# Doubles of two pairs as the unit of the main loop in a four-layer graph network kernel

## The chip, the cores and the metric

One core of a Trainium2 chip runs the whole kernel; the other cores do nothing. The metric is the device time of one execution in microseconds. The engines are called PE (matrix multiply), DVE (vector), ACT (activation), POOL (GpSimd) and SP (which issues most DMAs). Each works through its own instructions in order and waits for the others by semaphores.

## The reference

There are 128 graphs of 64 nodes with 128 features each (`x`), and one 64 x 64 matrix of edge distances per graph (`adj`), symmetric in its pattern, with about a quarter of its entries not zero. Four layers follow one another, each with a residual and a layer norm:

```python
# layer 0: continuous filter, 20 Gaussians, cosine cutoff
f_ij = exp(coeff * (d_ij[..., None] - offsets) ** 2)
rcut = 0.5 * (cos(d_ij * pi / CUTOFF) + 1.0) * (d_ij < CUTOFF)
W = (ssp(f_ij @ fw1 + fb1) @ fw2 + fb2) * rcut[..., None]
agg = einsum('bjf,bijf->bif', x @ w_in2f, W)
out = ssp(agg @ ow1 + ob1) @ ow2 + ob2

# layer 1: the same with 64 Gaussians; the edges are weighted with A * A
# layer 2: graph convolutions with the normalised adjacency
h = elu(elu(x @ W0 + b0))
h = elu(norm_A @ (h @ W1) + b1)
out = norm_A @ (h @ W2) + b2

# layer 3: out = relu((A_norm @ X) @ W.T + b)
# each layer: x = layernorm(x + out)
```

`ssp` is softplus minus log 2. In layers 0 and 1 the filter `W` is computed for every edge, which is nearly all the work. Everything is float32.

## The kernel before

**Tiling.** The graphs are sorted by their number of edges and taken in pairs: 64 pairs in 8 sets of 8. For each pair the edges are compacted into *slots*; the number of slots of a pair is fixed by its set (948 to 1092 in layer 0, 1140 to 1260 in layer 1, constant `GSLOTS`). Slots are ordered by the nodes they belong to, so that the sum over the edges of a node is a reduce over a stretch of neighbouring slots. The compaction of the first set is done ahead of the main loop; that of the later sets runs in small portions beside the loop (queues `early` and `side`), on DVE, POOL and through indirect DMAs.

**The loop.** `n` counts 128 pairs, 64 of layer 0 and then 64 of layer 1. A pair is cut into three steps of a third of its slots (316 to 364 columns in layer 0, 380 to 420 in layer 1; both graphs of a pair are handled in one step, so an ACT or DVE instruction has twice as many elements). A step is a pipeline over three iterations:

- `filter_in` (L1791): `px`, the matmul of the Gaussians `d` with the first filter weights, for two halves of 64 rows; then ACT's exponential into `h`. In layer 0 the three thirds of a pair lie on different rows of `d`, each with its own copy of the weights in `fw1`.
- `softplus`: ACT's logarithm of `h`, in place.
- `gather` (L1817), one iteration later: `pg`, the matmul of the node features with the selection matrix `hot`; then ACT's copy into `g`.
- `filter_out` (L1805), two iterations later: `pw`, the second filter matmul. All ACT instructions are recorded at L933.
- `message` (L1831): DVE computes `(pw + b2) * g` into the pair's messages `m`.
- `slot_sums` (L1854, L1858): 9 reduces on DVE from `m` into `agg`, once per pair, spread over the following steps.

`px`, `pg` and `pw` have one PSUM tile of two banks each, without a second buffer. So the next `px` waits for the exponential, the next `pg` for the copy and the next `pw` for the message. `one_hot` (L1779) builds `hot` on DVE from slot numbers and edge weights `w`.

**Beside the loop.** Pairs form groups of four (`GS`). A group's node work is in generators that yield between pieces; each step runs one piece of each queue: `befores` (features for the next group), `nodes` (`node_after`: `u` at L1581, softplus, `o`, un-sorting `back`, residual, layer norm) and the two queues `convs` (`graph_convs`: layers 2 and 3 of one group each, taken in turn by the group's number). In layer 0, `zero_share` adds what the entries with weight but no edge bring: a DVE instruction (L1554) adds it to `agg` just before `u`. Normal matrices of the convolutions are built by POOL (`scaled`, L1646) and transposed by PE (`nT`). POOL also does the layer norms' scaling (L1441) and scatters finished rows to the output. The last groups of layer 1 have 4, 2, 1 and 1 pairs, so that the end after the last step is short. The order of the instructions on each engine is the order in which this loop records them (`in_order`); the number of pieces of each queue at each step is written out by hand:

```python
        run(sums, ((1, 4, 4), (2, 4, 5))[n >= NP][k])
        run(early, 9 if i < 18 else (PACE - 2, PACE + 1, PACE + 1)[k] if i < 3 * (NP - 8) else 7)
        run(side, min(2, len(side)))
        run(stores, 1)
```

Loads of a pair (`d`, then `j` and `w`) are issued two pairs ahead: `d` at its step 0, `j` and `w` at step 1.

Of the kernel before, what the change touches and what calls it, by code (L numbers as in the profile page):

```python
# [19 lines left out]
P = 128  # L20
# [46 lines left out]
CHUNKS = tuple(tuple(n // 3 for n in sizes) for sizes in GSLOTS)  # L67
MAX_SLOTS, MAX_CHUNK = max(map(max, GSLOTS)), max(map(max, CHUNKS))

# [532 lines left out]
def sparse_stack(ctx: ExitStack, tc: tile.TileContext, t: dict, out: bass.AP, flag):  # L602
# [24 lines left out]
    dram = ctx.enter_context(tc.tile_pool(name="sscratch", bufs=1, space=DRAM))  # L627
    edge = ctx.enter_context(tc.tile_pool(name="sedge", bufs=2))
# [55 lines left out]
    columns = const.tile([P, P], F32, name="columns")  # L684
    column_i = const.tile([P, P], I32, name="column_i")
# [55 lines left out]
    def load_terms(name):  # L741
# [4 lines left out]
        yield  # L746
# [22 lines left out]
    fw1 = const.tile([P, 3, C], F32, name="fw1")  # L769
# [73 lines left out]

    def count(v, pool, total):
# [63 lines left out]
    caps_row = const.tile([1, NS, 2, 9], F32, name="caps_row")  # L908
# [7 lines left out]
    compacting = ctx.enter_context(ExitStack())  # L916
    cpt = compacting.enter_context(tc.tile_pool(name="scompact", bufs=1, side="right"))
# [377 lines left out]
    def bounded():  # L1295
# [11 lines left out]
        yield from wait_steps(8 * PACE)  # L1307
        for i, (w1, b1) in enumerate(loaded):
            nc.vector.scalar_tensor_tensor(w1, w1, -1.0, w1, ALU.mult, ALU.max)
            nc.vector.scalar_tensor_tensor(b1, b1, -1.0, b1, ALU.mult, ALU.max)  # L1310
            yield from wait_steps(2 * PACE)
            u = ps_n.tile([P, 512], F32, tag="n", name=f"sum_{i}")
            nc.tensor.matmul(u[:, 0:1], lhsT=w1, rhs=one[0 : w1.shape[0]], start=True, stop=True)
            nc.vector.tensor_add(b1, b1, u[:, 0:1])
# [3 lines left out]
    def settle():  # L1318
# [8 lines left out]
        yield from wait_steps(2 * PACE)  # L1327
        u = ps_n.tile([P, 512], F32, tag="n", name="odd_sum")
        nc.tensor.matmul(u[0:1, 0:3], lhsT=one, rhs=odds, start=True, stop=True)
        sums_ = const.tile([1, 3], F32, name="odd_sums")  # L1330
        nc.vector.tensor_copy(sums_, u[0:1, 0:3])
# [9 lines left out]
    def later_loads(n):  # L1341
# [9 lines left out]
        w = edge.tile([P, MAX_SLOTS], F32, tag="w", name=f"w_{n}")  # L1351
# [65 lines left out]
    def once(name, n, q):  # L1417

        if n < GS and rings:
            return tiled(name, n, q)  # L1420
        return node.tile([P, GS * P], F32, tag=name, name=f"{name}_{q}", bufs=1)[:, 0 : n * P]

    def layernorm(y, dst, n, name):

        stats = node.tile([P, GS, 6], F32, tag="st", name=f"st_{name}")[:, 0:n]
        mv = node.tile([P, GS, 2], F32, tag="mv", name=f"mv_{name}")[:, 0:n]
        for s in range(n):
            nc.vector.bn_stats(stats[:, s, :], y[:, s, :])
            nc.vector.bn_aggr(mv[:, s, :], stats[:, s, :])  # L1429
            if s + 1 == GS // 2 < n:  # L1430
                yield
        rstd = node.tile([P, GS], F32, tag="rs", name=f"rs_{name}")[:, 0:n]
# [624 lines left out]
```

## Time and profile before

| | us |
|---|---|
| median of 3 runs | 1589.59 |
| lowest and highest of them | 1589.56, 1591.46 |
| the profiled execution | 1576.21 |
| its span, first to last instruction | 1574.4 |
| PE, DVE, ACT, POOL busy in the span | 1435.9, 1365.7, 1335.9, 763.7 |
| first `px` of the main loop begins at | 67.9 |
| layer 0, pairs in eight sets | 67.9 to 726.4 |
| layer 1, pairs in eight sets | 726.4 to about 1500 |

The profile is of one execution, which was 13.4 us shorter than the median. Times inside it are counted from its first instruction. A row of the groups names the line, engine and operation, what is written and read, the shape, how many there are, the time that they keep the engine busy, the mean of one in ns, and the engine's idle time just before them with what ended it. One float32 matmul is recorded as two matmul rows. The chain of waits follows the end of the program back, at each step to what released it. PE's granted clock was 0.984 of full speed.

### The profile page before, as it was taken

To read this page: it belongs to the slowest core of one execution; us is meant where nothing else is said; L and a number is where in the kernel's file an instruction comes from. 1 tells how busy PE (TensorE), PEld (TensorE's weight loads), DVE (VectorE), ACT (ScalarE), POOL (GpSimd) and SP (SyncE) were. 2 spreads that over 40 slices of the span, in tenths; PEclk is the share of its full clock that TensorE was granted. 3 is DMA by queue.
4 is the path that set the end of the run, shared out by engine and by line. 5 is a ranking of instruction groups with operands and counts; after the bars stand their busy time and mean duration, and the time that the engine had idled before them with its cause. 6 is when DMAs were issued, how large, how long until landed. Compare 5 with 4: busy or idle time off the path is not lost.

```text
span 1574.4 us, 24209 instructions
## 1 busy us (share of the span) xinstructions
PE 1435.9 (91%) x6813; PEld 812.1 (52%) x6813; DVE 1365.7 (87%) x3549; ACT 1335.9 (85%) x1846; POOL 763.7 (49%) x1175
## 2 busy tenths in 40 slices
PE   1379999999999999999999999999999999999975
PEld 1134455555555555554445555555555655555554
DVE  8789999999999998889878888888888887898873
ACT  1369898989898988889999999999999998999952
POOL 2434356555655635335521346544565444664454
PEclk9999999999999999999999999999999999999985
DMA  6755455545454643437565455544555454555200
GB/s 207 256 132 145 128 125 148 129 128 141 121 140 122 151 125 100 129 100 185 142 151 130 122 148 131 144 124 124 137 134 138 120 132 128 131 143 132 70 8 23
DMA packets 122290, 205.68 MB, mean 131 GB/s; under 512 B 47956, under 2 KB 80034, under 8 KB 121506
## 3 DMA queue, kind: packets, MB, share of 16 engines
q1 hardware_dynamic: 113330, 188.40, 46.8%
q0 software_dynamic: 6576, 14.99, 2.8%
q8 instruction: 57, 0.93, 0.3%
q10 hardware_dynamic: 2240, 0.65, 0.2%
q14 instruction: 87, 0.71, 0.2%
HBM read 185.29 MB, written 18.64 MB: 130 GB/s over the span
## 4 chain that ended last, share of the span: by engine, by line
PE 33%; DVE 21%; POOL 13%; DMA 10%; ACT 9%; issue 6%; SPq 3%; DVEq 0%; POOLq 0%; ACTq 0%
PE pw L1805 12%; PE px L1791 7%; DVE m L1831 6%; PE pg L1817 5%; DMA out_dram<-gz,at_row 5%; POOL x_all L1441 5%; ACT h L933 4%; DVE agg L1854 4%; DVE hot L1779 2%; POOL rs L1436 2%; SPq L1354 2%; POOL gz L1441 2%; DMA w<-w_dram 2%; ACT g L933 2%; PE hw L1689 1%
## 5 line engine op out<-in xcount | busy, mean ns | idle before, releaser
L933 ACT ACTIVATE h<-h,half 128x672 f32<-128x672 f32 (+13 forms) x385 | 353.7, 919 | 0.1
L933 ACT ACTIVATE g<-pg 128x672 f32<-128x672 f32 (+12 forms) x384 | 303.8, 791 | 28.0 <-DVE m L1831 18.6
L1854 DVE TENSOR_REDUCE agg<-m 128x16 f32<-128x240 f32 (+13 forms) x896 | 319.6, 411 | 2.9
L1817 PE MATMUL pg<-hot,ys 64*128 64x336 f32 (+12 forms) x1536 | 308.8, 478 | 12.8 <-DVE hot L1779 9.6
L1805 PE MATMUL pw<-h,w_L_gnn_W2T 128*128 128x420 f32 (+5 forms) x768 | 306.2, 521 | 1.6 <-DVE m L1831 1.6
L1831 DVE SCALAR_TENSOR_TENSOR m<-pw,c_L_gnn_b,g 128x840 f32<-128x840 f32 (+5 forms) x192 | 201.3, 1048 | 104.5 <-PE pw L1805 95.4
L1805 PE MATMUL pw<-h,w_L_gnn_fw 128*128 128x336 f32 (+6 forms) x768 | 264.6, 467 | 21.3 <-DVE m L1831 20.1
L1805 PEld LDWEIGHTS pw<-h,w_L_gnn_W2T 128*128 128x128 f32 x768 | 130.3, 189 | 148.5 <-issue 32.6
L1831 DVE SCALAR_TENSOR_TENSOR m<-pw,c_L_gnn_fb,g 128x672 f32<-128x672 f32 (+6 forms) x192 | 176.9, 921 | 33.4 <-PE pw L1805 21.6
L933 ACT ACTIVATE h<-px,c_L_gnn_fb 128x672 f32<-128x672 f32 (+6 forms) x192 | 159.5, 830 | 53.5 <-PE px L1791 53.2
L1817 PEld LDWEIGHTS pg<-hot,ys 64*128 64x128 f32 x1536 | 146.0, 187 | 113.6 <-issue 17.8
L933 ACT ACTIVATE h<-px,c_L_gnn_b 128x840 f32<-128x840 f32 (+5 forms) x192 | 178.8, 931 | 26.0 <-PE px L1791 25.4
L1791 PE MATMUL px<-d,fw 64*128 64x336 f32 (+6 forms) x768 | 165.7, 506 | 28.9 <-ACT d L933 18.8
L1805 PEld LDWEIGHTS pw<-h,w_L_gnn_fw 128*128 128x128 f32 x768 | 132.8, 191 | 112.8 <-DVE m L1831 65.1
L1779 DVE SCALAR_TENSOR_TENSOR hot<-j,row,w 128x1212 f32<-128x1212 bf16 (+12 forms) x128 | 177.9, 1390 | 7.4 <-DMA d<-d_dram 7.4
L1791 PE MATMUL px<-d,w1t 64*128 64x420 f32 (+5 forms) x768 | 181.1, 548 | 1.1 <-ACT h L933 1.1
L1435 POOL TENSOR_SCALAR rs<-mv 128x4 f32<-128x4 f32 x61 | 14.7, 240 | 305.1 <-DVE mv L1429 303.1
L933 ACT ACTIVATE d<-d,neg_off 128x1212 f32<-128x1212 f32 (+12 forms) x128 | 120.3, 940 | 9.0 <-DMA d<-d_dram 9.0
L1791 PEld LDWEIGHTS px<-d,fw 64*128 64x128 f32 x768 | 59.5, 187 | 120.8 <-ACT h L933 48.9
L973 POOL DMA_INDIRECT rows<-comb,goes x64 | 67.8, 1060 | 96.7 <-DMA rows<-comb,goes 66.6
L1441 POOL TENSOR_SCALAR x_all<-ny,mv,rs 128x128 f32<-128x128 f32 x124 | 105.4, 859 | 3.3
L973 POOL DMA_INDIRECT out_dram<-gz,at_row x56 | 78.6, 1403 | 13.9 <-POOL blocks L1646 4.5
(262 smaller groups left out, 2243.8 us busy)
## 6 DMA issues: line engine op xcount, KB each, us to landing
d<-d_dram SPq DMA_DIRECT2D x32, 315.0 KB
w<-w_dram SPq DMA_DIRECT2D x32, 315.0 KB
d<-d_dram SPq DMA_DIRECT2D x32, 303.0 KB
w<-w_dram SPq DMA_DIRECT2D x32, 303.0 KB
w<-w_dram SPq DMA_DIRECT2D x32, 252.0 KB
j<-j_dram SPq DMA_DIRECT2D x32, 157.5 KB
j<-j_dram SPq DMA_DIRECT2D x32, 151.5 KB
d<-d_dram SPq DMA_DIRECT2D x16, 300.0 KB
```

The costliest lines, as they stand in the source:

```text
L933: latest = nc.scalar.activation(out_, in_, func, **kw)
L973: nc.gpsimd.indirect_dma_start(out=into, out_offset=bass.IndirectOffsetOnAxis(ap=at, axis=0), in_=rows, in_offset=None,)
L1354: engine.dma_start(to, dram_ap(slots[layer, name][s], first, [[0, to.shape[0]], [1, n]]))
L1436: nc.gpsimd.tensor_tensor(rstd, rstd, neg_half[:, 0:n], ALU.pow)
L1441: (nc.gpsimd if n == GS else nc.vector).tensor_scalar(dst[:, s, :], y[:, s, :], mv[:, s, 0:1], rstd[:, s : s + 1], ALU.subtract, ALU.mult,)
L1689: nc.tensor.matmul(ps[:, s, :], lhsT=lhs(s), rhs=rhs(s), start=True, stop=True)
L1779: nc.vector.scalar_tensor_tensor(hots[n][:, 0:size], j[:, 0:size], near, wt[:, 0:size], ALU.is_equal, ALU.mult)
L1791: nc.tensor.matmul(ps[:, b, 0:n], lhsT=w1, rhs=d[rows, col : col + n], start=True, stop=True)
L1805: nc.tensor.matmul(c["pw"][:, b, :], lhsT=c["w"]["w2"], rhs=c["h"][:, b, :], start=True, stop=True)
L1817: nc.tensor.matmul(ps[:, b, 0:n], lhsT=y[rows, :], rhs=hots[c["n"]][rows, at], start=True, stop=True,)
L1831: nc.vector.scalar_tensor_tensor(messages[n][:, :, at], c["pw"], c["w"]["b2"], c["g"], ALU.add, ALU.mult)
L1854: nc.vector.tensor_reduce(av[:, :, :, r], both, AX.X, ALU.add)
```

## The change

The unit of the loop becomes a *double* of two neighbouring pairs.

- **Steps.** In layer 1 a double is cut into 5 steps of about two fifths of a pair's slots (456 to 504 columns); the middle one takes the end of the first pair and the beginning of the second. In layer 0 a double is cut into 4 steps of half a pair where a pair has up to 1024 slots (sets 3 to 7, 474 to 510 columns), otherwise into 6 as before. `filter_in` and `gather` issue one pair of matmuls for each piece with its own weights or its own pair.
- **In place.** `hot` is written over `w` (three buffers instead of two). ACT copies `pg` straight into the double's messages `m`, and DVE multiplies there.
- **Sums.** The 9 reduces run once for a double, over twice as many elements each; only the last double is summed pair by pair. `agg` is single-buffered.
- **Zero share.** It is no longer added to `agg`: ACT writes the scaled share (`zz`), and `u` is computed in four matmuls, in layer 0 in four pairs of matmuls that accumulate share and sums. The share's work moves to the queue `befores`.
- **Turns.** How many pieces of each queue a step runs, and at which step loads and Gaussians are issued, comes from a table for 6, 5 and 4 steps. `graph_convs` of a large group waits for given steps of a group (`at_phase`), and `befores` runs at given steps alone. The two normal matrices are built within `elu` while ACT works. Some layer norms run in fewer pieces.

The core of the diff:

```diff
+def chunks_of(layer, size):
+    if layer == 1:
+        wide = -(-2 * size // 5)
+        return (wide, wide, size - 2 * wide, size - 2 * wide, wide, wide)
+    n = 2 if size <= 1024 else 3
+    return (size // n,) * (2 * n)
...
-        w = edge.tile([P, MAX_SLOTS], F32, tag="w", name=f"w_{n}")
+        w = edge.tile([P, MAX_SLOTS], F32, tag="w", name=f"w_{n}", bufs=3)
...
     def zero_share(q):
...
-        nc.vector.scalar_tensor_tensor(agg, ps, zero_filter, agg, ALU.mult, ALU.add)
+        shares[q] = once("zz", GS, q)
+        act(shares[q], flat, AF.Identity, scale=zero_filter)
...
-        nc.tensor.matmul(
-            u, lhsT=w["o1"], rhs=agg.rearrange("f s r -> f (s r)"), start=True, stop=True
-        )
+        for s in range(n):
+            of = agg[:, s, :]
+            if n > 1:
+                of = agg[:, s // 2 * 2 : s // 2 * 2 + 2, :].rearrange("f s r -> f (s r)")
+                of = of.rearrange("f (b s r) -> f s b r", b=2, s=2)[:, s % 2]
+            if layer == 0:
+                nc.tensor.matmul(by[:, s, :], lhsT=w["o1"], rhs=share[:, s, :], start=True, stop=False)
+            nc.tensor.matmul(by[:, s, :], lhsT=w["o1"], rhs=of, start=layer == 1, stop=True)
...
         if n == GS:
+            yield from at_phase(6)
             scaled(2, q)
...
-        hots[n] = edge.tile([P, MAX_SLOTS], F32, tag="hot", name=f"hot_{n}")
+        hots[n] = wt
...
+    def pieces(c):
+        at = 0
+        for part_ in c["parts"]:
+            first, stop = part_["cols"]
+            third = stop if c["layer"] else part_["all"] // 3
+            while first < stop:
+                k = first // third
+                end = min(stop, (k + 1) * third)
+                yield part_, k, first - k * third, at, end - first
+                at, first = at + end - first, end
...
+        for to, of in c["to"]:
+            act(to, ps[:, :, of], AF.Copy)
+
+    def message(c):
+        for to, of in c["to"]:
+            nc.vector.scalar_tensor_tensor(
+                to, c["pw"][:, :, of], c["w"]["b2"], to, ALU.add, ALU.mult
+            )
...
+        v = m.rearrange("f (g k) -> f g k", g=8 * pairs)
...
+    TURNS = {
+        6: dict(
+            sums=(1, 1, 2, 1, 2, 2), early=(PACE - 2, PACE + 1, PACE + 1) * 2, side=(2,) * 6,
+            late=(2, None, None, 3, None, None), load=(2, None, None, 3, None, None),
+            gauss=((1, 0), (1, 1), None, (2, 0), (2, 1), None),
+            end=(7,) * 6,
+        ),
+        4: dict(
+            sums=(2, 3, 2, 2), early=(6, 7, 6, 7), side=(2, 3) * 2,
+            late=(2, None, 3, None), load=(2, None, 3, None),
+            gauss=((1, 1), None, (2, 1), None),
+            end=(12, 13, 12, 13),
+        ),
+        5: dict(
+            sums=(2, 2, 1, 2, 2), early=(8, 8, 8, 9, 9), side=(2, 2, 2, 3, 3),
+            late=(2, None, None, 3, None), load=(2, None, 3, None, None),
+            gauss=((1, 1), None, (2, 0), (2, 1), (3, 0)),
+            end=(10,) * 5,
+        ),
+    }
+    FREE, MORE = 8, 0
+    BEFORES = {6: (3, 4, 7, 8, 9), 4: (2, 3, 5, 6, 7), 5: (7, 8, 9)}
```

## The prediction

> **What bounds the kernel now.** I read the busy table by stretches first, because the page's shares (PE 91%, DVE 87%, ACT 85%) average over stages with different limits; then the chain of waits in order of time in one stretch of each layer; then the groups kept apart by shape, for the price of one instruction.
>
> The stretches are eight pairs of layer 0 with 1008 slots, eight more with 996, eight pairs of layer 1, and the end. Columns: stretch, its length, then busy us of PE, weight loads, DVE, ACT and POOL.
>
> ```profile
> 409.00:489.00 80.00, 75.49 (x372) 41.81 (x370) 76.36 (x243) 71.07 (x107) 48.46 (x74) 1.00 0.56 139
> 569.00:651.00 82.00, 77.28 (x377) 43.10 (x378) 73.02 (x194) 70.41 (x107) 33.08 (x61) 0.98 0.43 117
> 1110.00:1207.00 97.00, 96.42 (x476) 56.74 (x472) 83.22 (x178) 91.02 (x116) 51.19 (x56) 1.00 0.50 132
> 1500.00:1574.40 74.40, 45.31 (x189) 33.06 (x185) 38.87 (x128) 25.42 (x71) 34.38 (x46) 0.70 0.06 16
> ```
>
> In layer 1 PE is idle 0.6 us of 97 and ACT 6; in layer 0 DVE and PE stand side by side with some 4 us idle each; in the end nothing is full. The chain says the same. Here is one step of layer 1 (420 columns) and the smaller pieces around it, then part of layer 0; columns are start, us, what.
>
> ```profile
> 1419.20 1.61 PE pw L1805 x4
> 1420.81 0.86 PE u L1581 x2
> 1421.67 0.89 PE hw L1689 x8
> 1422.56 0.91 PE px L1791 x4
> 1423.47 0.70 PE pg L1817 x4
> 1424.17 1.61 PE pw L1805 x4
> ...
> 413.68 0.91 DVE m L1831
> 414.58 0.50 DVE agg L1854 x2
> 415.09 0.54 DVE agg L1858 x2
> 415.63 0.64 DVE comb L1235 x5
> ```
>
> Layer 1 is an unbroken string of matmuls: PE is its bound. Layer 0 is mostly a string of DVE work: messages, slot sums and the compaction of later sets. Prices of one instruction come from two widths of the same operation (count, busy us, mean ns):
>
> ```profile
> L1854 DVE TENSOR_REDUCE agg<-m 128x16 f32<-128x176 f32 x48 | 15.7, 326 | 0.0
> L1854 DVE TENSOR_REDUCE agg<-m 128x16 f32<-128x352 f32 x24 | 12.2, 509 | 0.2
> L1831 DVE SCALAR_TENSOR_TENSOR m<-pw,c_L_gnn_fb,g 128x672 f32<-128x672 f32 x48 | 43.7, 909 | 5.3 <-PE pw L1805 3.1 <-ACT h L933 1.2 <-ACT nh L933 0.8
> L933 ACT ACTIVATE h<-h,half 128x672 f32<-128x672 f32 x48 | 41.2, 858 | 0.0
> L933 ACT ACTIVATE h<-px,c_L_gnn_fb 128x672 f32<-128x672 f32 x48 | 39.5, 822 | 12.5 <-PE px L1791 12.4
> L933 ACT ACTIVATE g<-pg 128x672 f32<-128x672 f32 x48 | 35.1, 731 | 5.5 <-DVE m L1831 3.0 <-PE pg L1817 2.2
> ```
>
> A reduce has 143 ns that do not depend on its width (326 minus 176 x 1.04). But in the chain two reduces of the same kind take 0.50 us where their durations add to about 0.66: an instruction's last 0.08 us lies over the next one. So a removed reduce returns about 0.06 us, a removed message about 0.09. On ACT the fixed parts from start to start are about 0.18 (logarithm), 0.14 (exponential) and 0.05 us (copy), 0.37 us for the three of a step.
>
> **The change part by part.** The bytes moved, the columns streamed and the elements handled stay the same; what changes is how many instructions carry them.
>
> *Steps.* Two pairs took 6 steps; they take 5 in layer 1 (32 doubles) and 4 in sets 3 to 7 of layer 0 (20 doubles), so 32 + 40 = 72 steps go. ACT loses 72 x 0.37 = 27 us (12 in layer 1, 15 in layer 0), DVE 72 x 0.09 = 6 us. On PE a step of 420 columns takes 0.91 + 0.70 + 1.61 = 3.22 us. Of this 2.8 is streaming: the four wide records of pw start 352 ns apart at 420 columns, and px and pg together stream as long as pw, since their two row halves run side by side. The other 0.42 is switching, half of it around pw. A removed pw block returns 0.2 us: 6.4 us in layer 1, 8 in layer 0. px and pg of layer 1 are not saved: the middle step is cut at the pair's end, so there are still six pieces of each. In layer 0 a half of a pair crosses a border between thirds, where the weights change: 8 pieces of px instead of 6, 40 more in all, 0.1 to 0.2 each, +6; 40 fewer of pg, -2 (bounds 0 and -4).
>
> *Slot sums.* One set of 9 reduces per double, not per pair: 567 fewer x 0.06 = 34 us off DVE, half in each layer.
>
> *Zero share.* Its 745 ns addition on DVE (16 times) goes: 16 x 0.66 = 10.5 us. ACT gets 16 scaled copies of 512 at the 0.6 us of its neighbours, +10. PE adds the share by accumulation: 16 matmuls of 128 columns in place of two records of 512. Eight records of 128 take 0.89 (hw), so 1.78 against 0.86: +0.92 x 16 = 15 us on PE in layer 0. Layer 1's u, cut in four, is 0.89 against 0.86: nothing.
>
> *In place.* The selection matrix overwrites its weights; the buffer is now held until the gather instead of until DVE has read it, but there are three. The load for the pair after next is issued one step earlier in the double and needed four steps (16 to 20 us) later, against 5 us to land: hidden; if that cover were gone, 5 us per pair. SP issues the same loads and is held at most until the gather of the same step; nothing urgent stands behind. The Gaussians' loads get two long steps instead of three short ones, both about 10 us. The messages in place end ACT's wait for g (28.0 us of idle time on the page's row, 18.6 behind DVE), mostly in layer 0; in return the first copy of each double waits for the last sums of the double two before. Between 0 and 1.5 us of ACT per double; I take 0, as ACT keeps idle time in both layers. agg has one buffer instead of two: the first sum of a group waits until u of the group before has been read, which PE does in the step before; behind it on DVE stand the selection matrix and the message that PE's next pw waits for. At most 1 us for each of 31 groups, at least nothing; I take 0, since a whole step lies between.
>
> *Turns.* Conv work is pinned to a step of its group, and the two normal-matrix steps move into the elu's waiting time. POOL has the same instructions in slightly another order. The trace does not show what this does: PE waits for sup and its weights some 16 us in all, so the gain has that bound; the loss is the second rival. I take 0.
>
> **The sum.** Layer 1: PE -6.4, and it has no other slack to give: -6. Layer 0, sets 3 to 7: DVE loses 4 x 9 x 0.06 + 8 x 0.09 + 2 x 0.66 = 4.2 us per set, but PE gains 1.8 (u) - 0.8 (steps) = +1.0. So PE takes over. At the 98% that it reaches in layer 1, the stretch at 409 goes to (75.5 + 1.0) / 0.98 = 78.1, -1.9; that at 569 to 79.9, -2.1; the five sets together give -7. Sets 1 and 2 keep six steps and get +1.8 on PE: by the same working -1.3 each. The first set hangs on its loads: 0. Layer 0: -9.5. End: 0. In all -15.5 on the profiled execution's 1576.2 (span 1574.4), so 1560.7. The median shown, 1589.6, stands 13.4 above it, and I keep that distance: 1574.
>
> [...] In layer 1 the rows show PE busy 96.4 of 97, weight loads 56.7, ACT 91.0. [...]
>
> **The rivals.**
> *More than that (15%).* [...]
> *PE gives nothing back in layer 0 (18%).* PE is already 94% busy there, and u costs it 15 us. Then only layer 1's 6 remain, less 1 to 4 for longer px switches: about -4, 1585; within reach of no change.
> *Slower: the turns send conv work into the end (17%).* Sums now finish a double later, and a conv that has missed its step waits up to ten steps (48 us of a group). In the changed program the conv of the last-but-one large group begins some 5 steps before the loop's end, about 25 us, where it began 12 steps (45 us) before. Its and the next group's POOL work (two layernorms of some 5 us each, four scatters of 1.4 us and up to 4.5 to land) then queue one after another in the end, where POOL is busy 34 of 74 us. It decides once this chain ends after that of the very last pair; at the full 20 us, and with layer 0 giving nothing, it is +14: 1604. Against: the last pair's chain alone takes most of the 74 us, and two links of the large groups' chain are gone.
> That the number of steps does not fall is excluded: the changed program has 72 fewer of each step's instructions.
>
> **How the numbers follow.** Main case 50%: 1574, own range 1567 to 1581. About 0.2% (3.2 us) is what a measurement here can tell from no change. Faster: 0.50 + 0.15 + half of the second rival = 0.74; same 0.09; slower 0.17. The range leaves out the outer half of the first and of the last rival: 1556 to 1596.
>
> **What would show it.** Right: step intervals in sets 3 to 7 with PE at 97% or more and DVE under 93%; u in layer 0 at about 1.8 us; layer 1's eight pairs at 96 to 97 instead of 97 to 98; the end at 72 to 78 us. Wrong: PE's idle time in layer 0 stays at 4 us or more a set, ACT waiting for agg's reduces before its first copy of a double, or an end over 85 us.

## The result and the profile after

The changed kernel takes 1576.39 us (median of 4 runs, 1575.13 to 1580.1) against 1589.80 for the kernel before: ratio 0.9917, 95% interval 0.9899 to 0.9936. Measured again later, it took 1580.92 beside 1587.65: 0.9947 (0.9930 to 0.9965), a gain of 6.7 us where the first was 13.4. The forecast was 1574 in a range of 1556 to 1596, a gain of 15.5. The time came out; most of the working behind it did not, and that the parts add up to nearly the forecast is luck, as the last part shows.

The profiled execution has a span of 1575.4 us. Here are its busy times by stretches; the columns are again stretch, length, and busy us of PE, weight loads, DVE, ACT and POOL, then PE's granted clock, DMA share and GB/s. The first two rows answer to the stretches of 1008 and 996 slots, the third to layer 1. The last two split the final stretch at the end of the last `pw`: the last eight pairs, and the end after them.

```profile
424.10:505.50 81.40, 74.89 (x369) 38.52 (x368) 76.06 (x221) 69.13 (x86) 48.03 (x77) 1.00 0.55 133
...
584.00:658.50 74.50, 73.13 (x373) 38.72 (x372) 65.31 (x127) 68.86 (x86) 37.88 (x64) 1.00 0.52 133
...
1099.60:1194.20 94.60, 94.60 (x471) 55.03 (x470) 80.92 (x139) 89.09 (x105) 50.16 (x56) 1.00 0.55 136
...
1380.20:1510.80 130.60, 117.39 (x539) 65.92 (x539) 102.72 (x193) 99.95 (x123) 66.68 (x87) 0.95 0.31 78
1510.80:1575.40 64.60, 36.39 (x168) 28.52 (x166) 30.79 (x105) 20.33 (x60) 30.00 (x38) 0.68 0.06 18
```

The same last eight pairs before:

```profile
1400.90:1509.40 108.50, 106.52 (x496) 59.76 (x495) 94.83 (x203) 96.90 (x125) 60.43 (x77) 1.00 0.38 96
```

Three readings. In layer 0 the gain is uneven: the stretch of 1008 slots is no shorter than before (81.4 us for 80.0, PE 6.5 us idle), that of 996 is 7 us shorter. In layer 1 PE is busy for the whole of the stretch, which is 2.8 us shorter. And the last eight pairs are 22 us longer, 11 of them PE's idle time and 11 its busy time. The end after the last `pw` is as it was (65.0 before, 64.6 after).

From the pages, first the chain that ended last by engine, after the change; then ACT's copy before and after (busy, mean ns | idle just before, releasers):

```profile
PE 61%; ACT 11%; DVE 9%; DMA 6%; issue 4%; SPq 2%; POOL 2%; another core or an unknown queue 1%; DVEq 0%; ACTq 0%; POOLq 0%
...
L933 ACT ACTIVATE g<-pg 128x672 f32<-128x672 f32 (+12 forms) x384 | 303.8, 791 | 28.0 <-DVE m L1831 18.6
...
L955 ACT ACTIVATE m<-pg 128x1008 f32<-128x1008 f32 (+12 forms) x313 | 291.8, 933 | 46.1 <-DVE agg L1916 21.0
```

PE's share of the chain was 33% before. ACT's wait before its copy was 28.0 us, mostly for the message; now it is 46.1, mostly for the sums of an older double.

The whole by stages, us from the first `px` of one set to that of the next (sets of eight pairs, numbered from 0 in each layer in the order in which they run; "end" is what follows the last set). Two executions stand for the kernel before: one without, one with a stall in set 0 that is told of at the end.

| | L0 set 0 | L0 1-2 | L0 3-7 | L1 0-1 | L1 2-6 | L1 7 and end | span |
|---|---|---|---|---|---|---|---|
| before, first profile | 93.6 | 166.6 | 398.3 | 185.2 | 489.3 | 173.5 | 1574.4 |
| before, again | 107.1 | 166.5 | 399.4 | 185.2 | 491.1 | 172.1 | 1589.5 |
| after | 102.4 | 174.3 | 384.9 | 178.1 | 472.9 | 195.2 | 1575.4 |
| after, again | 104.1 | 174.3 | 385.1 | 178.1 | 472.8 | 197.2 | 1579.3 |
| six steps in layer 0 | 103.5 | 174.3 | 420.9 | 173.4 | 472.8 | 191.5 | 1603.9 |
| six steps in layer 1, turns fixed | 104.7 | 173.6 | 383.8 | 195.6 | 565.3 | 190.8 | 1681.2 |
| six steps in layer 1, turns free | 103.3 | 172.4 | 387.5 | 202.1 | 520.7 | 184.3 | 1638.0 |
| turns free | 95.1 | 173.3 | 381.0 | 182.9 | 486.4 | 178.6 | 1565.4 |
| sums by pair | 98.5 | 179.4 | 403.7 | 184.5 | 480.1 | 190.9 | 1604.4 |
| share on DVE, just before `u` | 103.7 | 177.8 | 401.7 | 177.3 | 472.8 | 196.7 | 1597.8 |
| share on DVE, behind the sums | 94.4 | 172.2 | 385.1 | 185.1 | 472.8 | 196.4 | 1574.1 |
| two conv turns a step at the end | 93.5 | 173.3 | 381.8 | 178.2 | 472.8 | 206.5 | 1573.9 |
| last 16 pairs free | 103.3 | 175.5 | 385.3 | 178.1 | 483.6 | 178.5 | 1572.0 |
| the same, Gaussians split | 104.6 | 173.4 | 434.5 | 177.9 | 483.6 | 179.8 | 1621.4 |

The runs were on several chips, and set 0 depends on the chip. The stages behind it do so less: where sets 3 to 7 of layer 0 are as in the changed kernel, they take 381.0 and 381.8 us in the rows without the stall and 383.8 to 387.5 in those with it, so a difference of 3 us there between two chips says nothing. Stages are compared with the rows "after", or with a row of the same chip where that is said, and ratios with the kernel before on the same chip.

### The profile page after: what moved, and what is told of

It is laid out like the page before. It is cut to its first block, busy times and chain, and to the rows that moved or that the text cites. A ratio compares the mean times of both kernels' runs of the same rounds, so it can differ in the third digit from the quotient of the medians.

```text
span 1575.4 us, 23201 instructions
## 1 busy us (share of the span) xinstructions
PE 1427.4 (91%) x6841; PEld 790.8 (50%) x6841; DVE 1316.5 (84%) x2895; ACT 1313.8 (83%) x1647; POOL 759.3 (48%) x1175
## 4 chain that ended last, share of the span: by engine, by line
PE 61%; ACT 11%; DVE 9%; DMA 6%; issue 4%; SPq 2%; POOL 2%; another core or an unknown queue 1%; DVEq 0%; ACTq 0%; POOLq 0%
PE pw L1842 23%; PE px L1827 13%; PE pg L1856 11%; ACT h L955 5%; DVE m L1882 2%; DMA w<-w_dram 2%; DVE agg L1912 2%; DMA j<-j_dram 2%; ACT d L955 2%; PE y L1491 1%; PE hw L1722 1%; SPq L1378 1%; PE u L1615 1%; PE back L1641 1%; PE o L1632 1%
## 5 line engine op out<-in xcount | busy, mean ns | idle before, releaser
L955 ACT ACTIVATE h<-h,half 128x1008 f32<-128x1008 f32 (+12 forms) x313 | 332.8, 1063 | 0.1
L955 ACT ACTIVATE m<-pg 128x1008 f32<-128x1008 f32 (+12 forms) x313 | 291.8, 933 | 46.1 <-DVE agg L1916 21.0
L1856 PE MATMUL pg<-w,ys 64*128 64x504 f32 (+15 forms) x1376 | 299.4, 518 | 27.0 <-ACT d L955 7.5
L1842 PE MATMUL pw<-h,w_L_gnn_W2T 128*128 128x504 f32 (+8 forms) x640 | 300.2, 592 | 2.6 <-DVE m L1882 2.4
L1882 DVE SCALAR_TENSOR_TENSOR m<-pw,c_L_gnn_b,m 128x1008 f32<-128x1008 f32 (+8 forms) x161 | 194.8, 1211 | 113.6 <-PE pw L1842 97.7
L1912 DVE TENSOR_REDUCE agg<-m 128x32 f32<-128x544 f32 (+14 forms) x455 | 287.2, 669 | 1.8 <-PE u L1615 0.4
L1842 PE MATMUL pw<-h,w_L_gnn_fw 128*128 128x504 f32 (+6 forms) x608 | 253.6, 540 | 9.7 <-DVE m L1882 7.7
L955 ACT ACTIVATE h<-px,c_L_gnn_b 128x1008 f32<-128x1008 f32 (+8 forms) x160 | 171.4, 1071 | 30.2 <-PE px L1827 30.0
L1803 DVE SCALAR_TENSOR_TENSOR w<-j,row,w 128x1212 f32<-128x1212 bf16 (+12 forms) x128 | 181.3, 1416 | 5.4 <-DMA w<-w_dram 5.4
L1827 PE MATMUL px<-d,w1t 64*128 64x504 f32 (+11 forms) x768 | 173.1, 542 | 0.5 <-ACT h L955 0.4
```

What stands on the lines that cost most here:

```text
L955: latest = nc.scalar.activation(out_, in_, func, **kw)
L1803: nc.vector.scalar_tensor_tensor(hots[n][:, 0:size], j[:, 0:size], near, wt[:, 0:size], ALU.is_equal, ALU.mult)
L1827: nc.tensor.matmul(ps[:, b, at : at + m], lhsT=w["w1"][rows, :] if c["layer"] else w["w1"][rows, k, :], rhs=d[rows, col : col + m], start= ...
L1842: nc.tensor.matmul(c["pw"][:, b, :], lhsT=c["w"]["w2"], rhs=c["h"][:, b, :], start=True, stop=True)
L1856: nc.tensor.matmul(ps[:, b, to], lhsT=y[rows, :], rhs=hots[part_["n"]][rows, first:stop], start=True, stop=True,)
L1882: nc.vector.scalar_tensor_tensor(to, c["pw"][:, :, of], c["w"]["b2"], to, ALU.add, ALU.mult)
```

## The experiments

**The kernel before, beside itself.**

> The kernel before, unchanged, once more. The profiled execution of before was 1576.2 us where its timed ones were 1589.6, and the changed kernel's profiled one was 1577.3 where its timed ones were 1576.4. If the 13 us are the luck of one execution, this profile has a span near 1588 and shows which stretch is longer than in the first; if profiling itself shortens this kernel, the span is near 1574 again and the timed runs stay at 1590. Ratio to before 1.000 either way.

Measured: 1588.91 us, ratio 0.9991 (0.9975 to 1.0007). Its profile has a span of 1589.5 us, so it was not profiling that made the first one shorter. The 13 us that the first profile lacked lie in set 0 (107.1 for 93.6). On which chip the first profile was taken is not on record.

**Six steps in layer 0.** Everything else is as changed.

```diff
-    n = 2 if size <= 1024 else 3
+    n = 3
```

> The changed kernel with layer 0 in 6 steps throughout. Prediction: sets 3 to 7 gained some 7 us, of which the steps are about half (0.8 us of PE per set, 0.7 us of DVE, 3 us of ACT): the total rises by 4 us, to 1580. Rival (long steps bring nothing where PE and DVE are both nearly full): within 2 us of the changed kernel, 1576. Second rival (long steps of layer 0 harm by coarser waits): 3 to 8 us faster than the changed kernel.

Measured: 1605.34 us, ratio 1.0082 (1.0048 to 1.0116). Sets 3 to 7 take 420.9 us in place of 384.9, of which the next set returns 4.7: four steps instead of six are worth about 31 us there, with the rest of the change in place. Of these, with the next two sets counted in, 22 are PE's busy time (some of it at a lower granted clock, 0.96 to 1.00 by set) and 9 its idle time. But 420.9 is also 21.5 us above the kernel before, and sets 1 and 2, which have six steps in both, are 7.8 above it. So by difference the rest of the change costs layer 0 some 25 us, and the steps more than pay for it. How much of that is the table of turns for six steps, which was written for sets 0 to 2, was not tried. PE's waits in sets 3 to 6 of this kernel (engine, line, what it waited for: us in all, times, longest):

```profile
PE pw L1842 <- DVE m L1882: 8.3, 11, 1.9
PE pg L1856 <- ACT h L955: 4.6, 5, 1.1
PE pg L1856 <- issue: 3.9, 3, 3.1
PE pg L1856 <- ACT d L955: 2.9, 7, 0.8
PE px L1827 <- ACT h L955: 2.8, 4, 0.7
PE zs L1578 <- ACT zt L955: 2.4, 7, 1.0
```

Beside `pw`, which waits for the message as it did before (7.6 us in these sets), stand waits for ACT: behind the exponential (`ACT h`), behind the Gaussians (`ACT d`) and behind the copy of `zt` for the share.

**Six steps in layer 1, turns fixed.** The cut of a double in layer 1 is three steps to a pair. The table of turns for six steps is the one of layer 0, with `end` at 9 and the last sums spread over six steps.

```diff
-    if layer == 1:
+    if False:
...
-    n = 2 if size <= 1024 else 3
+    n = 2 if layer == 0 and size <= 1024 else 3
...
-        if layer == 1:
-            cuts[2:4] = [cuts[2] + cuts[3]]
```

> The changed kernel with layer 1 in 6 steps of a third of a pair per double (and so small changes of how many background pieces a step runs), all else kept. Theory A (the steps: fewer and longer steps save switching on PE and hand-overs between engines): the five middle sets of layer 1, 16.6 us shorter in the changed kernel's profile than before, go back to 96 to 99 us each, and the total rises by 6 (the switching alone, as predicted) to 20 us, to 1582 to 1597. Theory B (the fixed conv turns and the in-place messages made layer 1 faster): those sets stay at 93 to 96 us and the total rises by less than 5 us.

Measured: 1679.37 us, ratio 1.0558 (1.0518 to 1.0599). This says little of steps, for the turns are at the same numbers (6 and 2) in a group of twelve steps instead of ten. They now meet the scatters, as the waits of one set (115 us) show:

```profile
POOL out_dram L995 <- DMA out_dram<-gz,at_row: 16.7, 6, 3.4
...
ACT gy_hw L955 <- DMA out_dram<-gz,at_row: 9.0, 2, 4.7
...
PE gh L1750 <- ACT gy_hw L955: 5.7, 2, 3.0
```

ACT's copy for a conv waited up to 4.7 us for a scatter to land, and `gh` on PE up to 3.0 us for that copy. So the cut was tried again without turns.

**Free turns.**

```diff
     def at_phase(k):
-        while phase[0] not in (k, None):
-            yield
+        return
+        yield
```

> As the changed kernel, but the convolutions of a large group wait for no given step; they go on at the next turn. Theory 'the turns hold conv work back': the 22 us that the last eight pairs got longer come from convs that wait for their step. Then layer 1's middle sets get up to 3 us longer each, and the last eight pairs with the end go from 195 to 175-185 us; in all 1565-1574. Rival 'the order of the last eight pairs': their length comes from work of the groups of two and one that meets there, whatever the turns: the last stretch stays at 190-200, the whole within 4 us of the changed kernel's 1576. Rival 'the turns protect PE's queue': PE waits for scatters or for POOL in the middle sets again; 2 to 4 us more in each, 1590 or more.

Measured: 1567.53 us, ratio 0.9956 (0.9939 to 0.9973). This chip is faster: the kernel before takes 1574.67 there and set 0 has no stall. The expectations for this run, for the sums by pair, for the share behind the sums and for two conv turns, which ran on the same chip, reckon from 1576. On this chip the changed kernel was not run; the kernel with two conv turns at the end, told of below, differs from it in the last stretch alone and gets there at 1367.4, so with a last stretch of 195 to 197 us the changed kernel would take an estimated 1565, 0.994 of the kernel before. Free turns are thus some 3 us slower, not 9 faster. Sets 2 to 6 of layer 1 take 13.6 us more than with fixed turns, 2.7 each; the first two 4.8 more; the last with the end 16.6 to 18.6 less. So both the first theory and the last hold in part: the turns hold conv work back, and they keep PE's queue clear while they do. In sets 2 to 6 PE idles 8.0 us with free turns, 7.3 of them in waits for ACT's `xt`, and not at all with fixed ones. PE's waits in one set of 1200 slots with free turns:

```profile
PE o L1767 <- ACT xt L955: 0.8, 1, 0.8
PE hw L1722 <- ACT xt L955: 0.6, 1, 0.6
```

and in the kernel before, where the five sets have 3.7 us of this kind and 4.7 us of idle time in all:

```profile
PE sup L1689 <- POOL x_all L1441: 0.9, 3, 0.3
```

**Six steps in layer 1, turns free.** Both edits together.

> As the kernel with free turns, but layer 1 in six steps a double, three to a pair (sums and the last steps spread over six; selection matrix, messages and sums as changed). Theory 'a removed step returns PE time': 32 steps more at 0.5-0.65 us, as measured in layer 0: 16 to 21 us more than with free turns and five steps, 2 to 2.7 in each middle set. The prediction's own price is 0.2 us a step, 6 us in all. Rival 'in layer 1 the turns made the gain, not the steps': within 3 us of the kernel with free turns.

Measured: 1639.31 us, ratio 1.0324 (1.0293 to 1.0355). Sets 2 to 6 take 34.3 us more than with five steps and free turns: 20 steps more, 1.7 us each. The 0.5 to 0.65 expected was three times too small, the prediction's 0.2 eight times. In the five sets 13.7 of the 34.3 us are PE's busy time and 20.6 its idle time. One set of 1200 slots in this kernel and in the one with free turns:

```profile
1037.90:1143.20 105.30, 99.63 (x487) 56.68 (x486) 82.32 (x143) 93.15 (x116) 49.45 (x56) 1.00 0.48 125
```

```profile
999.50:1098.10 98.60, 96.98 (x473) 55.01 (x472) 81.64 (x139) 91.20 (x105) 49.69 (x57) 1.00 0.52 133
```

Of the 6.7 us, 2.7 are PE's work and 4.1 are its idle time (5.7 against 1.6). The largest wait behind that in the six-step set is for messages:

```profile
PE pw L1842 <- DVE m L1882: 2.9, 4, 1.2
PE pg L1856 <- ACT gy_hw L955: 1.1, 1, 1.1
```

The kernel before also has six steps and takes 489.3 for these sets, 31 less than this one. So the parts do not add: with the rest of the change in place, six steps are much worse than they were before, and five a little better. Which part makes it so is not shown: sums by doubles, messages in place, one `agg`, or the table of turns for six steps, which could perhaps be placed better. So the 34 us are the worth of the steps within this program, not in general.

**Sums by pair.** Sums run once a pair, over half as many elements, and a step runs about twice as many. The layout of `m` and of `u`'s operand follows (not shown).

```diff
-            sums=(1, 1, 2, 1, 2, 2),
+            sums=(2, 3, 3, 2, 3, 3),
...
-            sums=(2, 3, 2, 2),
+            sums=(4, 5, 4, 5),
...
-            sums=(2, 2, 1, 2, 2),
+            sums=(3, 4, 3, 4, 4),
...
-            (n, size), pairs = (part_["n"], part_["all"]), 1 if c["n"] == N - 2 else 2
+            (n, size), pairs = (part_["n"], part_["all"]), 1
```

> As the changed kernel, but slot sums run once for each pair, over half as many elements, at twice the pace. 567 more reduces, at 0.06 us returned by each some 34 us more of DVE, half in each layer. Theory 'each stage has its own bound': in layer 1 and in sets 6 and 7 of layer 0 PE is busy 98% or more and hides it; in sets 1 to 5 (DVE 70-76 of 78-88 us busy) 2 to 4 us each: 1584-1596. Rival 'the sums of a double come in a lump and stand before the message': with smaller pieces PE's wait for messages shrinks and the run is even or faster, 1570-1577.

Measured: 1605.48 us, ratio 1.0186 (1.0152 to 1.0221): above the range of either theory. Against the kernel with two conv turns at the end, which ran beside it, layer 0 loses 33 us and sets 0 to 6 of layer 1 another 14. DVE's busy time rose by 40.2 us (1356.4 for 1316.2), 0.07 for each of 567 reduces, and the kernel lost no less than that, although DVE was 90% busy or less in each set and PE 99% in sets 2 to 6 of layer 1. The way to PE is seen in layer 0: in sets 3 to 6 `pw` waits 11.4 us for the message, 1.6 in the kernel beside it. In layer 1 it is another: PE's only waits in sets 2 to 6 are 4.7 us for `xt`, while DVE waits 48 us for `pw`. How the sums delay `xt` was not followed.

**The share on DVE, just before `u`.** DVE adds the share to `agg` in two additions of 256 columns for a group, and `u` is one matmul to a pair again.

```diff
-            if layer == 0:
-                nc.tensor.matmul(by[:, s, :], lhsT=w["o1"], rhs=share[:, s, :], start=True, stop=False)
-            nc.tensor.matmul(by[:, s, :], lhsT=w["o1"], rhs=of, start=layer == 1, stop=True)
+            nc.tensor.matmul(by[:, s, :], lhsT=w["o1"], rhs=of, start=True, stop=True)
```

> The changed kernel with the zero share added on DVE again (two additions of 256 columns per group of layer 0, about 0.35 us each, from the copy that ACT has scaled), and u in four matmuls without accumulation: PE loses 16 x 0.9 = 15 us of work in layer 0, DVE gains 16 x 0.7 = 11 us. Prediction (PE is what limits layer 0 after the change): 5 to 12 us faster than the changed kernel, 1565 to 1571. Rival (DVE still limits layer 0): 2 to 8 us slower. Second rival (both are coupled and neither matters): within 2 us.

Measured: 1600.72 us, ratio 1.0072 (1.0043 to 1.0101). Sets 3 to 7 take 16.8 us more. One wait alone is larger than that; PE in sets 3 to 7:

```profile
PE u L1619 <- DVE agg L1613: 22.5, 10, 4.0
```

`u` stood at once behind an addition that was itself behind DVE's queue. If that is a price of the place, another place avoids it.

**The share on DVE, behind the sums.** The same additions, given out behind the group's last reduce.

```diff
         if s + pairs == agg.shape[1]:
+            if layer == 0:
+                share = by_pair(shares.pop(q))
+                for d in range(2):
...
+                    nc.vector.tensor_add(of, of, part_)
+                yield
```

> As the changed kernel, but DVE adds the zero share to the sums (two additions of 256 columns for each group of layer 0) right behind the group's last reduces, a step or so ahead of u, and u takes one matmul for each pair. PE loses 16 x 0.92 = 15 us, DVE gains some 11. An earlier kernel with the same additions right before u was 24 us slower. Theory 'PE waited for the addition because of its place': now sets 6 and 7 lose 1.9 us each, sets 1 to 5 between 0 and 2: 1566-1574. Rival 'DVE has no room for it': 1585-1600 again.

Measured: 1573.62 us, ratio 0.9994 (0.9978 to 1.0010). The 22.5 us wait is gone, but the 15 us taken from PE are not gained: sets 3 to 7 take 385.1 us, 3.3 more than in the kernel with two conv turns beside it, and the next two sets 6.9 more. The figure lies in the first theory's range only because the chip is faster; against the estimated 1565 it is 9 us slower. Neither theory holds: moving the additions removed that wait, but the kernel is still slower than with the share on PE. Had sets 6 and 7 returned what PE was spared, they would have lost 4 us. Set 7 lost 1.0 (69.7 for 70.7), and set 6 grew by 2.5 (77.0 for 74.5): PE is busy 0.8 us less there and idle 4.6 us instead of 1.4, in a wait of 2.0 for ACT and one of 1.5 for DVE. DVE had the additions in exchange, so the run shows that this move does not pay, and not that less work for PE would bring nothing.

**Two conv turns a step in the last eight pairs.**

```diff
-    FREE, MORE = 8, 0
+    FREE, MORE = 8, 8
```

> As the changed kernel, but in the last eight pairs of layer 1 each convolution queue gets two turns a step. Theory 'conv work of the last two large groups comes too late': it now ends earlier; last eight pairs and end 195 to 180-190, whole 1563-1573. Rival 'conv pieces stand in the way of the steps': two pieces a step make the steps longer, 1578-1590. Rival 'the very last pair's chain sets the end': within 3 us of 1576.

Measured: 1577.12 us, ratio 1.0011 (0.9997 to 1.0024). The last stretch grows from 195-197 to 206.5 us, the whole is 12 us above the estimated 1565; that it stands within 3 us of 1576 comes from the faster chip. The second reading holds: conv pieces stand in the way of steps. PE's waits in the last eight pairs of this kernel:

```profile
PE hw L1722 <- DVE er L1669: 7.6, 4, 2.5
PE sup L1722 <- POOL x_all L1466: 7.2, 3, 6.1
```

Two pieces of one chain in one step leave no step between them, so PE waits for what lies between the first and the second. That is a reading of these waits; it was not tried apart.

**The changed kernel again, beside the next.**

> The changed kernel itself, beside the others of this call. The kernel before is 1590 us on one chip and 1575 on another; the difference is a stall of all engines in the first set. If the changed kernel loses less in that stall (its first set was 5 us shorter), its ratio on a chip without the stall is nearer to one, about 0.9935 (1564 beside 1575); if the stall is nothing to do with the gain, 0.992 on any chip.

Measured: 1580.92 us, ratio 0.9947. That chip has the stall too (set 0 takes 104.1 us), so the question about a chip without it stays open; the estimate for one is 0.994.

**The last sixteen pairs free.**

```diff
-    FREE, MORE = 8, 0
+    FREE, MORE = 16, 0
...
-        if layer == 1 and befores and (n >= N - 8 or phase[0] in BEFORES[beat]):
+        if layer == 1 and befores and (phase[0] is None or phase[0] in BEFORES[beat]):
```

> As the changed kernel, but the last sixteen pairs, not eight, run without fixed turns. Without fixed turns anywhere the middle sets of layer 1 took 2.8 us more each and the last eight pairs with the end 16.6 us less. Theory 'fixed turns save PE time in every set and put some conv work off to the end': the set before the last takes up the work put off, 98-101 us in place of 92.6, and the last stretch comes down to 178-182; 6 to 10 us less than the changed kernel in all. Rival 'the end is long because the groups' convs start late by a fixed time': the last stretch stays above 190 and the whole at or above the changed kernel.

Measured: 1574.08 us (1573.35 to 1576.14), ratio 0.9919 (0.9892 to 0.9946), beside 1580.92 (1577.09 to 1581.93) of the changed kernel on the same chip: 6.8 us less, and no run of one reaches the other. The set before the last takes 103.4 us instead of 92.7, the last stretch 178.5 instead of 197.2. The last eight pairs of this kernel:

```profile
1393.50:1507.00 113.50, 108.52 (x506) 59.87 (x506) 99.72 (x186) 97.05 (x119) 68.80 (x85) 1.00 0.35 88
```

PE idles 5.0 us there instead of 13.2, and works 108.5 us instead of 117.4 (there the granted clock was 0.95, here 1.00). This is the best version found that was run beside both kernels.

**The same with the Gaussians split.** In the doubles of four steps one Gaussian instruction a step, not two every other step.

```diff
-            gauss=((1, 1), None, (2, 1), None),
+            gauss=((1, 0), (1, 1), (2, 0), (2, 1)),
```

> As the kernel whose last sixteen pairs run without fixed turns, and in the doubles of four steps the Gaussians' two ACT instructions of 0.58 us are given out one at each step, not two at every other step. In sets 3 to 7 PE waits 3.8 us for a copy behind the Gaussians and 3.2 behind the exponential. Theory 'lumps of ACT work in front of the gather's copy keep PE waiting': sets 3 to 5 lose 1 to 3 us each, sets 6 and 7 (PE busy 98-100%) nothing; 2 to 6 us less than 0.9919 of the kernel before, 0.988 to 0.9907. Rival 'PE waits for the same chain a step later': sets 3 to 5 within 1 us of 79.6, 80.7 and 79.8, ratio 0.991 to 0.993.

Measured: 1623.25 us, ratio 1.0198 (1.0173 to 1.0222). Both theories fail: sets 3 to 7 take 49.2 us more. PE's waits in sets 3 to 6:

```profile
PE px L1827 <- ACT d L955: 34.7, 23, 5.0
PE px L1827 <- DMA w<-w_dram: 2.9, 2, 1.9
```

ACT in one double (start us, us, then engine, line and shapes):

```profile
453.92 1.14 ACT L955 ACTIVATE h<-h,half 128x1008 f32<-128x1008 f32 x1
454.95 0.60 ACT L955 ACTIVATE ys<-y 128x512 f32<-128x512 f32 x1
455.43 0.58 ACT L955 ACTIVATE d<-d,coeff 128x336 f32<-128x336 f32 x1
457.29 1.10 ACT L955 ACTIVATE h<-px,c_L_gnn_fb 128x1008 f32<-128x1008 f32 x1 [1.28 <-PE px L1827]
```

The second instruction for a pair now comes last in the step just before that pair's first `px`. PE waits for it, up to 5.0 us, and then ACT waits for `px` (1.28 us). The lump of two had left a whole step of slack; the spread took it away. Here the distance of an instruction to its reader counted for more than its length.

## Why the prediction was right, and where it was not

**The sum: right by luck.** From stage to stage, against the kernel before with the stall ("before, again"), in us:

| | L0 set 0 | L0 1-2 | L0 3-7 | L1 0-1 | L1 2-6 | L1 7 and end | in all |
|---|---|---|---|---|---|---|---|
| forecast | 0 | -2.6 | -7 | -1.5 | -3.8 | -0.8 | -15.5 |
| measured | -4.7 | +7.8 | -14.5 | -7.1 | -18.2 | +23.1 | -14.1 |

(The forecast's -6 for layer 1 is divided evenly over its eight sets, and its terms are rounded; half a microsecond of the measured change lies ahead of set 0.) No stage is near its forecast, and the errors cancel. Layer 0 alone, 11.9 us earlier at its end (729.2 against 741.1) where -9.5 was forecast, holds up to 5 us of a smaller stall in set 0. Without the stall, in the kernel with two conv turns against the first profile, it is 10.0: set 0 gives nothing and sets 3 to 7 give 16.5. Layer 1 with the end takes only 2.2 us less (846.2 against 848.4), and in the second execution of the changed kernel 0.3.

**Steps, mis-sized.** The forecast let a removed step of layer 1 return only the 0.2 us around `pw`, and priced layer 0's pieces at +6 for `px` and -2 for `pg`. The blocks show otherwise. Layer 1 before, at 400 columns, from the chain of waits:

```profile
1031.94 0.87 PE px L1791 x4
1032.81 0.67 PE pg L1817 x4
```

The `pw` ahead of them took 1.54 us: 3.08 for the three. After, at 480 columns in layer 1, and at 474 in layer 0:

```profile
1009.27 1.01 PE px L1827 x4
1010.28 0.81 PE pg L1856 x4
1011.08 1.82 PE pw L1842 x4
...
702.88 1.00 PE px L1827 x8
703.88 0.80 PE pg L1856 x4
...
705.26 1.59 PE pw L1842 x4
```

6 x 3.08 = 18.5 against 5 x 3.64 = 18.2: 0.3 us a double, or 1.1 to 1.2 a set where the forecast said 0.8. And a `px` of two pieces (x8, 474 columns) takes 1.00 us, no more than one piece of 480: the border between thirds costs nothing that shows. Layer 0's steps are 3.39 us. So PE got lighter in layer 0, by 1.3 to 2.7 us a set (74.0, 74.9, 74.1, 73.1 and 70.6 in sets 3 to 7 against 76.6, 76.2, 76.0, 75.3 and 73.3), with a `u` that is longer by the predicted 1.8, and not heavier by 1.0: this is the step of the prediction that failed most plainly. Without `u`, PE lost 3.1 to 4.5 us a set, some 0.4 to 0.55 for each removed step, where the forecast had 0.1. PE's busy time is no fixed amount, though: with sums by pair it had the same matmuls as the kernel with two conv turns beside it and was busy 8.5 us longer in all (1434.3 for 1425.8), so a part of the gain can be smoother running.

**What the steps are worth whole** is larger still: some 31 us in layer 0 and 34 in five sets of layer 1, as the two six-step kernels show within this program. PE's idle time is 9 of the 31 us and 20.6 of the 34; the rest is its busy time. The prediction priced a step by PE's own instructions, mostly by the 0.2 us around `pw`, and the waits that a longer step hides at nothing.

**`u`: right.** 0.92 us a group was predicted. In a late group of layer 0:

```profile
646.12 0.42 PE u L1614 x2
646.54 0.22 PE u L1615 x2
646.76 0.22 PE u L1614 x2
...
647.88 0.22 PE u L1615 x2
```

The eight entries take 1.98 us from 646.12 on, or 1.78 without the 0.2 by which the first is longer. What was to follow from it was not seen: giving the share back to DVE brought nothing.

**"PE takes over" in layer 0: not shown.** The reading of the lines, DVE and PE side by side with some 4 us idle each, holds for the stretch of 1008 slots; in that of 996 DVE had 9.0 us idle and PE 4.7. After the change PE is at 92 to 94% in sets 3 to 5, below the 97% that was to show it right, and at 98 to 100% in sets 6 and 7. The sign for wrong, 4 us or more of PE's idle time, stands in sets 3 to 5 (5.8, 6.5 and 4.4 us) and not in 6 and 7 (1.4 and 0.1). These two gained 10.6 us, where the forecast's rule gives 2.1 for set 6 and nothing for set 7; sets 3 to 5 gained only 4. DVE's other work runs out here (127 instructions in set 6, 221 in set 4), so the long strings of DVE work that the chain showed before are gone; that this is the cause was not tried.

**Slot sums, mis-sized.** The forecast's 0.06 us a reduce is 34 us off DVE, and the page is near it: with messages and the share DVE lost 49.2 us (1365.7 to 1316.5), 50.5 predicted; undoing the sums alone adds 40.2. But it took most of them as covered by PE, and undoing them costs some 46 us up to the last stretch. In layer 0 DVE, 80 to 94% busy in sets 1 to 7, is on the path through the message that frees `pw`; in layer 1 the path was not followed.

**Sets 1 and 2: wrong sign.** -1.3 each was predicted; they take 7.8 us more (+1.8 and +6.0). They have the costs and not the steps, and the six-step kernel of layer 0 shows the same in the other sets: about 3 us a set, of which `u` is 1.8. The costs taken at nothing are the rest. One of them is seen: "ACT waiting for agg's reduces before its first copy", a sign for wrong, is the 21.0 us on the page, 11.1 of them in sets 3 to 6. How much of the loss comes from it, from the sums' place or from the Gaussians' place stays open; separate buffers for the copies or the sums were not tried.

**Layer 1: the steps nearly as priced, the turns at nothing.** Sets 2 to 6 gained 16.4 us (489.3 to 472.9); the forecast had 4. By the blocks above the steps are 6 of them. Some 8 are `sup`: before, PE idled 4.7 us in these sets, mostly for it, and its matmuls took 14.4 us; after, PE does not idle and they take 10.5. With free turns both are gained too, but PE idles 8.0 us for other things, is busy 478.4 us instead of 472.9, and only 2.9 us are left. So the turns, priced at nothing, made 13.6 us. The bound of 16 that the forecast set for them rested on waits for `sup`, which vanish with free turns as well; that 13.6 comes near it is chance. The eight pairs were to take 96 to 97 us and take 94.6.

The lower end of the forecast's range, 1556, counts on 15 us from layer 1, a term that no run shows. What the runs show in its place is 16.4 us in sets 2 to 6 with fixed turns, 6 of them from the steps by the blocks above, and 2.9 with free turns, where ACT had lost the same instructions; that 15 is near 16.4 is chance. In the stretch of 94.6 us weight loads are busy 55.0 and PE is busy throughout, in one unbroken string of blocks, and the stretch is as long as they are.

**The rival with the turns: its amount came, not its place.** It put +20 into the end, because convs begin later. They hardly do: the last but one large group's `gx` starts at 1462.6, 48 us before the last `pw` ends, where the forecast had 25; before it was 1455.0, 54 before. The end has its 64.6 us. But the last eight pairs are 22 us longer. Some 7 of these are work moved there from set 1 of layer 1, which shortens by as much (stretch, length, then busy us of PE, weight loads, DVE, ACT and POOL; before, then after):

```profile
815.10:911.60 96.50, 96.14 (x455) 53.92 (x454) 82.26 (x161) 93.02 (x117) 31.89 (x37) 1.00 0.52 134
818.10:907.30 89.20, 88.81 (x401) 46.08 (x400) 75.67 (x107) 88.12 (x100) 25.58 (x30) 1.00 0.60 143
```

PE has 54 fewer instructions there, and in the second execution of the changed kernel 55 more in the last stretch (705 for 650), while sets 2 to 6 have nearly the same number. So the 7.1 us that sets 0 and 1 gained are no gain. Freeing the turns one set earlier takes 18.7 us off the last stretch for 10.8 in the set before; of the 5.0 us by which the last eight pairs are then still longer than before (113.5 against 108.5), PE's work is 2.0 and its idle time 3.0. Layer 1's middle paid for the rest, so the rival did not decide the sign.

**The offset, half right.** The 13.4 us between the profiled execution and the median were kept. They belong to set 0, as the next section shows, and the change shortened that set by some 3 to 5 us without aiming at it.

## What to carry to other kernels

Price a longer step by the waits that it hides as well as by the instructions that it saves: here the saved instructions of layer 0 were mis-sized four times over, and going back to six steps cost 30 us and more in each layer, some 30% of it in idle time of PE in the one and 60% in the other. Undo one part at a time before its price is believed, and remember that such a price holds with the other parts in place: the kernel before had six steps too and was far better with them than this one. When work is moved from a full engine to another, count the new waits that the other's readers get. Where work is held to fixed turns, see what is left over when the turns stop, and free them earlier: this was the cheapest gain of the study, 6.8 us for two lines.

## What the runs showed of the hardware

**A stall that depends on the chip.** The kernel before takes 1574.67, 1587.65, 1590.77 and 1592.49 us on four chips, with all runs of one chip within 0.7% of its median. In the profiles from the three slower ones set 0 is 9 to 13.5 us longer, and PE, DVE and ACT stand nearly still at about 145 us, while POOL and SP go on issuing DMAs. Waits between 134 and 165 us in the kernel before, second profile:

```profile
DVE m L1831 <- issue: 11.6, 1, 11.6
ACT h L933 <- remote: 8.6, 1, 8.6
...
PE pw L1805 <- issue: 6.1, 1, 6.1
...
PE zs L1552 <- issue: 4.0, 1, 4.0
```

and in the changed one:

```profile
DVE m L1882 <- remote: 9.9, 1, 9.9
ACT h L955 <- PE pw L1842: 6.6, 1, 6.6
```

With free turns, on the fastest chip, set 0 takes 95.1 us and no single wait there exceeds 2.1; the first profile of the kernel before has none above 1.4. "issue" and "remote" name nothing that the profile shows; what the engines wait for was not found. Of the gain measured on such a chip, 3 to 5 us are this stall.

**PE's granted clock was halved after some waits.** In set 2 of the changed kernel, where the set got longest (88.0 us for 82.0), the granted clock is 0.5 for 6.8 us from about the end of a wait of 2.3 us that `pw` had for the message (that `pw` took 2.80 us, the one ahead of it 1.39), and in set 3 for 3.4 us after one of 2.2. Waits of 1.3 to 1.7 us in sets 1 to 7 left it at 1.0. In the kernel with six steps in layer 0 it is 0.96 to 0.98 on average in three of sets 3 to 7, in sets 6 and 7 of the changed kernel 1.00. So a wait of some 2 us cost more than its own length there. Not every one did, and where the border lies was not measured: in the changed kernel one of 2.0 us, in the last eight pairs, left the clock at 1.0, and in the first profile of the kernel before one of 1.8 in set 6 of layer 0 brought it down to 0.5 for 3.4 us; the `pw` behind it took 2.50 us, the one ahead of it 1.39.
